# Graph network on one core: the search for slot starts on 125 partitions, with one row tile in its first group and the load of x moved ahead of the weights

## The chip, the core and the metric

The kernel runs on one core of a Trainium2 chip. The core has a matrix engine (PE, with its weight loads listed as PEld), a vector engine (DVE), a scalar engine (ACT), GpSimd (POOL) and a sync engine (SP) that here only issues DMAs. SP and ACT each have a hardware DMA queue; POOL has a software queue, used here for indirect gathers. All of them feed the same 16 DMA engines. Operands lie in an on-chip memory of 128 partitions, and matmul results in PSUM banks.

The metric is the device time of one execution in microseconds (us). The median of three runs before the change is 1657.53 us (1656.67 to 1657.77). The profiled execution took 1656.98 us; its instructions cover a span of 1655.2 us, so 1.8 us lie around the span. A change of less than 0.2% (3.3 us) can't be told from none.

## The reference

There are 6250 nodes with 64 features and 200,000 edges `(src, dst)`, sorted by `dst`, with 16 attributes each.

```
mean = segment_sum(x[src], dst) / max(count, 1)          # two SAGE layers
h    = relu(mean @ W_l1.T + b_l1 + x @ W_r1.T)
out  = mean(h) @ W_l2.T + b_l2 + h @ W_r2.T
x    = layernorm(x + out)
...                                                      # then three message layers
m    = concat([x[dst], x[src], edge_attr]) @ W.T + b
h    = relu(segment_sum(m, dst))                         # a batchnorm and a relu between layers
x    = layernorm(x + h)
```

Every layer sums over the neighbours of a node, with the same edges.

## The kernel before

**The plan.** The kernel turns the edges once into a dense matrix of counts (fp8, in 13 column tiles of 512 destinations; `adj8` in HBM), and each layer is then a matrix product with it (`aggregate`, L650). To build a tile (`build`, L920), the sorted edges are cut into windows of a few destinations. A window owns some *slots* of 128 edges. For a slot, DVE makes two one-hot matrices (L620: `lo` from the source, `rhs` from source and destination), PE multiplies them into a PSUM bank (L958), and ACT writes the counts out as fp8 (L965, L970). 128 slots share one *row tile* `t`: one indirect gather fetches 128 edges for each of the 128 slots (`rows`, L886), and DVE, ACT and PE make keys of it (L893 to L905). There are 21 row tiles (`R = 21`).

**The search.** For the gather, each slot needs the position of its first edge. Source and destination are packed into one integer per edge (`combine`, L791 and L792) and stored to HBM as one list, `cmb_d` (L797). The edges lie as 128 partitions of 1562, and the 64 left over form a rest `tl`, loaded, packed and stored by itself (L778, L779, L798). Four samples per partition (`smp`) are compared with every slot's threshold (`thr`, L815), PE counts the samples below (L820), and DVE turns the count into the position of the nearest sample by six small operations (L822 to L827). That is `near_samples`. An indirect gather then fetches the block of 456 edges behind the sample (L829), DVE counts in it (L838) and adds up the start (L840 to L842): `first_edges`. Row tiles are searched in five groups, `SEARCH`, of 3, 5, 5, 5 and 4 (the last of the 22 columns holds the starts for the edge attributes). An entry `(a, b, t0, t1)` says: group `a..b` takes its samples when row tile `t0` is reached, and finishes when `t1` is reached.

**The rest of the front.** `load_weights` (L585) issues 25 DMAs on SP, transposes the weights on PE (L589) and copies them out on ACT (L590). Behind it, x is loaded into `res` on SP: L872 for the 48 whole blocks of 128 nodes (1536 KB in rows of 256 bytes), L873 for the last 106 nodes. `split` (L626) divides x into three bf16 parts, in 13 pieces of four blocks (the last has one): two ACT casts and three DVE operations each (L629 to L633). The first `first_layer` product needs all 13.

**Order.** A planner places each engine's instructions, mostly as soon as it takes their inputs to be ready; `pin` keeps an instruction behind everything written before it for its engine. Pinned before the change are the comparisons L815, the gathers L829 and L886 and the counts L838. Each engine then runs its queue strictly in order.

**The bias.** `first_layer` adds `b_l2` to `res` (L729), once per tile. The loop over tiles of the second SAGE layer (L1064) reads `res` at L1073.

```
SEARCH = ((0, 3, 0, 0), (3, 8, 1, 2), (8, 13, 3, 4), (13, 18, 4, 5), (18, 99, 5, 6))
            search(0)
            load_weights()
```

Of the kernel before, what the change touches and what calls it, by code (L numbers as in the profile page):

```python
# [22 lines left out]
P = 128  # L23
# [393 lines left out]
SEARCH = ((0, 3, 0, 0), (3, 8, 1, 2), (8, 13, 3, 4), (13, 18, 4, 5), (18, 99, 5, 6))  # L417
NEAR = 456
# [58 lines left out]
def gnn_kernel(ctx: ExitStack, tc: tile.TileContext, x, src, dst, ea, W_l1, b_l1, W_r1, W_l2, b_l2, W_r2,  # L477
# [19 lines left out]
    EC1 = E // P  # L497
    TAIL = E - EC1 * P

# [21 lines left out]
    assert PADE >= P * EAG * 0 and EC1 * P + TAIL == E  # L521
# [30 lines left out]
    with ExitStack() as fast:  # L552
# [153 lines left out]
        def first_layer(psa1, a, j):  # L706
# [17 lines left out]
            for i in range(nb):  # L724
# [4 lines left out]
            nc.vector.tensor_tensor(res[:, bs: bs + nb, :], res[:, bs: bs + nb, :],  # L729
                                    bl2.unsqueeze(1).to_broadcast([P, nb, D]), ALU.add)  # L730
# [3 lines left out]
        with ExitStack() as bld:  # L734
# [19 lines left out]
            cmb = scratch[:, : 4 * EC1].bitcast(I32)  # L754
            sr = scratch[:, 4 * EC1: 8 * EC1].bitcast(I32)
            thr = scratch[:, 8 * EC1: 8 * EC1 + 4 * P * (R + 1)].bitcast(F32)
            most = max(min(b, R + 1) - a for a, b, *_ in SEARCH)
            size = 2 * NSMP * P * most
            less = [room[:, i * size: (i + 1) * size].bitcast(BF16).rearrange("p (q s) -> p q s", q=NSMP) for i in range(2)]
# [11 lines left out]
            tl = pp.tile([TAIL, 2], I32, name="tl")  # L771
            nc.sync.dma_start(cmb, dst[0: EC1 * P].rearrange("(p c) -> p c", p=P))
            nc.scalar.dma_start(sr, src[0: EC1 * P].rearrange("(p c) -> p c", p=P))
            t_ap = t_dram.ap() if hasattr(t_dram, "ap") else t_dram
            early = SEARCH[0][1] * P
            nc.scalar.dma_start(thr[:, :early], t_ap[:, :early].to_broadcast([P, early]))
            nc.scalar.dma_start(thr[:, early:], t_ap[:, early:].to_broadcast([P, P * (R + 1) - early]))
            nc.scalar.dma_start(tl[:, 0:1], dst[EC1 * P:].rearrange("(p c) -> p c", c=1))  # L778
            nc.scalar.dma_start(tl[:, 1:2], src[EC1 * P:].rearrange("(p c) -> p c", c=1))  # L779
            nc.scalar.dma_start(tab, c_dram.ap() if hasattr(c_dram, "ap") else c_dram)  # L780
            nc.scalar.dma_start(etab, e_dram.ap() if hasattr(e_dram, "ap") else e_dram)
            nc.gpsimd.memset(pad, 8191 << SBITS | TAG)
            one = pp.tile([P, 1], BF16, name="one")
            nc.gpsimd.memset(one, 1.0)

            gap = -(-EC1 // NSMP)
            smp = pp.tile([P, NSMP], I32, name="smp")
            every = slice(0, (NSMP - 1) * gap + 1, gap)

            def combine(to, d_, s_):  # L790
                nc.vector.tensor_scalar(to, d_, TAG >> SBITS, SBITS, ALU.bitwise_or, ALU.logical_shift_left)  # L791
                nc.vector.tensor_tensor(to, to, s_, ALU.bitwise_or)  # L792
# [3 lines left out]
            combine(tl[:, 0:1], tl[:, 0:1], tl[:, 1:2])  # L796
            nc.sync.dma_start(cmb_d[0: EC1 * P, :].rearrange("(p c) o -> p (c o)", p=P), cmb)  # L797
            nc.scalar.dma_start(cmb_d[EC1 * P: E, :], tl[:, 0:1])  # L798
            nc.scalar.dma_start(cmb_d[E: NCMB, :].rearrange("(p c) o -> p (c o)", p=64), pad[:64, :])

            blks = [spare(NEAR).bitcast(I32) for _ in range(most)]
            junk = spare(NEAR // 2).bitcast(BF16)
            ci = pp.tile([P, R + 1], I32, name="ci")
            cp = pp.tile([P, R + 1], I32, name="cp")
# [4 lines left out]
            def near_samples(g):  # L809


                t0, t1 = SEARCH[g][0], min(SEARCH[g][1], R + 1)
                s, n = slice(t0, t1), (t1 - t0) * P
                for q in range(NSMP):
                    pin(nc.vector.tensor_scalar(less[g % 2][:, q, :n], thr[:, t0 * P: t1 * P],  # L815
                                                smp[:, q: q + 1].bitcast(F32), None, ALU.is_gt))
                c1 = psm.tile([P, R + 1], F32, name="lin")
                for t in range(t0, t1):
                    for q in range(NSMP):
                        nc.tensor.matmul(c1[:, t: t + 1], less[g % 2][:, q, (t - t0) * P: (t - t0 + 1) * P], one,  # L820
                                         start=(q == 0), stop=(q == NSMP - 1))
                nc.vector.tensor_scalar(ci[:, s], c1[:, s], -1.0, 0.0, ALU.add, ALU.max)  # L822
                nc.vector.tensor_single_scalar(cp[:, s], ci[:, s], 2, ALU.logical_shift_right)
                nc.vector.tensor_single_scalar(ci[:, s], ci[:, s], NSMP - 1, ALU.bitwise_and)
                nc.vector.tensor_single_scalar(near[:, s], cp[:, s], float(EC1), ALU.mult)
                nc.vector.scalar_tensor_tensor(near[:, s], ci[:, s], float(gap), near[:, s], ALU.mult, ALU.add)
                nc.vector.tensor_copy(pos[:, s], near[:, s])  # L827
                for t in range(t0, t1):
                    pin(nc.gpsimd.indirect_dma_start(  # L829
                        out=blks[t - t0], out_offset=None, in_=cmb_d[:, :],  # L830
                        in_offset=bass.IndirectOffsetOnAxis(ap=pos[:, t: t + 1], axis=0)))

            def first_edges(g):

                t0, t1 = SEARCH[g][0], min(SEARCH[g][1], R + 1)
                s = slice(t0, t1)
                for t in range(t0, t1):
                    pin(nc.vector.tensor_scalar(junk, blks[t - t0].bitcast(F32), tab[:, 0, t: t + 1], None,  # L838
                                                ALU.is_lt, ALU.add, accum_out=c2[:, t: t + 1]))
                nc.vector.tensor_add(near[:, s], near[:, s], c2[:, s])  # L840
                nc.vector.tensor_add(near[:, s], near[:, s], tab[:, 1, s])
                nc.vector.tensor_copy(start_i[:, s], near[:, s])  # L842
# [12 lines left out]
            def search(t):  # L855
                for g, (_, _, t0, t1) in enumerate(SEARCH):
                    if t == t1:
                        if t0 == t1:
                            near_samples(g)
# [3 lines left out]
                for g, (_, _, t0, t1) in enumerate(SEARCH):  # L863
                    if t == t0 < t1:
                        near_samples(g)

            search(0)
            load_weights()


            nc.vector.memset(res[:, NB - 1, :], 0.0)
            nc.sync.dma_start(res[:, : NB - 1, :], x[0: (NB - 1) * P, :].rearrange("(b p) d -> p b d", p=P))  # L872
            nc.sync.dma_start(res[:LASTB, NB - 1, :], x[(NB - 1) * P:, :])  # L873
            nc.gpsimd.memset(parts[0][:, :, 3 * D: 3 * D + 1], 1.0)
            for b in range(0, NB, 4):
                nb = min(4, NB - b)
                split(parts[0][:, b: b + nb, :], res[:, b: b + nb, :], nb)
# [3 lines left out]
            def columns(t):  # L881
# [7 lines left out]
                if t:  # L889
                    search(t)  # L890
# [173 lines left out]
            for j in range(NT):  # L1064
# [8 lines left out]
                nc.vector.tensor_add(v[:, :nb, :], v[:, :nb, :], res[:, bs: bs + nb, :])  # L1073
                layer_norm(res[:, bs: bs + nb, :], v[:, :nb, :], nb)
# [155 lines left out]
```

## Time and profile before

| View | Value |
|---|---|
| Median of 3 runs | 1657.53 us |
| Profiled execution | 1656.98 us |
| Its span | 1655.2 us, mean granted PE clock 0.964 |
| Busy in the span | PE 1496.9, PEld 1379.9, DVE 920.0, ACT 578.4, POOL 117.0 us |
| Chain that ended last | PE 62%, DVE 21%, ACT 7%, issue 5%, DMA 3% |
| `dst` issued on SP, first DVE operation on it | 0.74 us, 6.95 us |
| Packed edges stored (L797 issued) | 12.93 us |
| First block gather (L829), first row gather (L886) | 23.29 us, 31.17 us |
| First key operation (L893), first one-hot (L620) | 38.09 us, 40.78 us |
| First slot product (L958) | 42.18 us |
| DVE operations of the splits of x | 46.42 to 70.5 us |
| Additions of `b_l2` (L729) | 13, of 0.42 us, from 145.1 to 622.3 us |

The page divides the span into 40 slices of 41.4 us; the front with which the change deals is the first of them, and the building of the matrix ends near 600 us. Busy times of single instructions overlap a little on DVE. A transfer's time from issue to landing includes its place in the queue.

### The profile page before, as it was taken

How to read it: one execution, taken by the hardware profiler on the slowest of the kernel's cores; microseconds unless marked ns; L12 is line 12 of the kernel's file. 1: busy time of each engine (PE TensorE's matmuls, PEld its weight loads, DVE VectorE, ACT ScalarE, POOL GpSimd, SP SyncE). 2: the span in 40 equal slices, each digit the busy share in tenths (PEclk: the TensorE clock that was granted, in tenths of full speed). 3: DMA queues.
4: the chain of work that ended last, by engine and by line, in shares of the span. 5: the costliest groups of instructions: out<-in, count | busy, mean ns of one | idle time of the engine just before them, and what ended most of it. 6: DMA issues, size and time to landing. Idle time of an engine off the chain costs nothing.

```text
span 1655.2 us, 38577 instructions
## 1 busy us (share of the span) xinstructions
PE 1496.9 (90%) x17135; PEld 1379.9 (83%) x17135; DVE 920.0 (56%) x1581; ACT 578.4 (35%) x1088; POOL 117.0 (7%) x72
## 2 busy tenths in 40 slices
PE   1586789899998989999999999999999999999997
PEld 0475668788887779889999888888899999899997
DVE  2999999998898733897888610001340100442122
ACT  1625466776885721454455300000220000310000
POOL 2024200360001010000000000000000000000000
PEclk9697899999999999999999999999899999899999
DMA  5021332032130373344534444442324542345450
GB/s 163 11 107 55 110 96 85 12 154 83 80 157 2 150 287 159 137 150 183 200 133 142 172 165 179 187 173 99 156 117 197 197 194 99 157 178 227 164 186 10
DMA packets 43811, 228.10 MB, mean 138 GB/s; under 512 B 22978, under 2 KB 30210, under 8 KB 35826
## 3 DMA queue, kind: packets, MB, share of 16 engines
q1 hardware_dynamic: 37058, 139.54, 22.4%
q10 hardware_dynamic: 4496, 79.48, 12.2%
q0 software_dynamic: 2080, 6.52, 1.3%
q8 instruction: 136, 2.23, 0.5%
q14 instruction: 41, 0.34, 0.1%
HBM read 183.76 MB, written 41.75 MB: 136 GB/s over the span
## 4 chain that ended last, share of the span: by engine, by line
PE 62%; DVE 21%; ACT 7%; issue 5%; DMA 3%; ACTq 0%; POOL 0%; DVEq 0%; POOLq 0%
PE agg L650 47%; DVE lo L620 7%; PE pair L958 6%; DVE rhs L620 4%; ACT a L965 4%; PE u L1110 2%; PE bank L1025 2%; DVE e L1016 1%; PE agg L657 1%; DVE e L1018 1%; DMA e<-in_edge_attr_dram 1%; DVE nd L675 1%; PE tr L700 1%; PE lin L1131 1%; DMA a<-adj 1%
## 5 line engine op out<-in xcount | busy, mean ns | idle before, releaser
L650 PE MATMUL agg<-parts,a 128*128 128x192 bf16 (+1 forms) x12005 | 1089.8, 246 | 5.6 <-DVE nd L675 1.8
L650 PEld LDWEIGHTS <-a 128*128 128x128 fp8e3 x12005 | 1008.3, 98 | 23.6 <-issue 12.1
L965 ACT ACTIVATE a<-pair 128x784 fp8e3<-128x784 f32 (+3 forms) x355 | 292.3, 890 | 122.8 <-PE pair L958 121.2
L958 PE MATMUL pair<-rhs,lo 128*128 128x147 bf16 (+5 forms) x2569 | 266.2, 244 | 64.0 <-DVE lo L620 30.3
L958 PEld LDWEIGHTS <-lo 128*128 128x128 bf16 x2569 | 196.2, 104 | 119.4 <-issue 52.1
L620 DVE TENSOR_TENSOR rhs<-iota,k 128x1960 bf16<-128x1960 f16 (+15 forms) x240 | 238.9, 1015 | 13.6 <-ACT k L905 11.3
L620 DVE TENSOR_TENSOR lo<-iota,k 128x2048 bf16<-128x2048 f16 x161 | 194.5, 1215 | 0.0
L675 DVE TENSOR_REDUCE z<-agg 128x256 f32<-128x768 f32 (+1 forms) x39 | 35.3, 910 | 282.7 <-PE agg L650 282.4
L620 DVE TENSOR_TENSOR lo<-iota,e_d 128x2048 bf16<-128x2048 f16 (+11 forms) x132 | 130.7, 1010 | 20.6 <-PE bank L1025 19.8
L1025 PE MATMUL bank<-lo,lhs 128*128 128x128 bf16 x1701 | 107.5, 219 | 17.4 <-ACT lhs L1019 12.1
L1025 PEld LDWEIGHTS <-lhs 128*128 128x128 bf16 x1701 | 98.4, 98 | 28.6 <-ACT lhs L1019 19.4
L675 DVE TENSOR_REDUCE nd<-agg 128x256 f32<-128x768 f32 (+1 forms) x26 | 23.4, 904 | 116.0 <-PE agg L650 116.0
L886 POOL DMA_INDIRECT rows<-cmb_d,start_i x21 | 64.8, 3084 | 207.4 <-ACT key L897 167.0
L1118 DVE BATCH_NORM_STATS2 stats<-hr 64x6 f32<-64x512 f32 (+1 forms) x26 | 17.0, 653 | 101.7 <-ACT hr L1133 80.4
L702 ACT COPY mx<-tr 128x512 f32<-128x512 f32 (+1 forms) x26 | 14.6, 562 | 166.9 <-PE tr L700 166.8
L691 ACT ACTIVATE sp_r<-z 128x256 f32<-128x256 f32 (+1 forms) x26 | 10.5, 403 | 171.4 <-DVE z L690 171.4
L1147 ACT ACTIVATE hr<-tr 64x512 f32<-64x512 f32 (+1 forms) x13 | 7.4, 566 | 179.9 <-PE tr L1146 179.9
L1015 ACT CAST lhs<-e 128x512 bf16<-128x512 f32 (+21 forms) x72 | 36.1, 502 | 59.6 <-PE bank L1025 44.6
L1126 POOL TENSOR_TENSOR nd<-res,inv 128x256 f32<-128x256 f32 (+1 forms) x13 | 7.6, 589 | 550.5 <-DVE ln_s L688 339.2
L1019 ACT CAST lhs<-e 128x512 bf16<-128x512 f32 (+21 forms) x72 | 36.4, 505 | 23.1 <-DVE e L1018 22.6
L1016 DVE TENSOR_TENSOR e<-e,lhs 128x512 f32<-128x512 f32 (+21 forms) x72 | 39.4, 550 | 8.9 <-ACT lhs L1015 8.8
L1017 ACT CAST lhs<-e 128x512 bf16<-128x512 f32 (+21 forms) x72 | 36.3, 504 | 22.2 <-DVE e L1016 21.0
(140 smaller groups left out, 819.6 us busy)
## 6 DMA issues: line engine op xcount, KB each, us to landing
a<-adj SPq DMA_DIRECT2D x24, 3136.0 KB, 12.4
a<-adj ACTq DMA_DIRECT2D x24, 3136.0 KB, 11.5
adj<-a SPq DMA_DIRECT2D x12, 3136.0 KB, 9.6
e<-in_edge_attr_dram SPq DMA_DIRECT2D x25, 256.0 KB, 2.7
a<-adj SPq DMA_DIRECT2D x4, 784.0 KB, 4.2
out_dram<-z SPq DMA_DIRECT2D x12, 128.0 KB, 6.5
a<-first_edges ACTq DMA_DIRECT2D x1, 1216.0 KB
e<-in_edge_attr_dram SPq DMA_DIRECT2D x7, 152.0 KB, 3.3
```

What stands on the lines that cost most here:

```text
L620: nc.vector.tensor_tensor(to.rearrange("p g (h two) -> p g h two", two=2), iota[:, :n].rearrange("p (h two) -> p h two", two=2).unsqueeze( ...
L650: nc.tensor.matmul(sums[k][:, i, :n], views[k][:, b, i * P: (i + 1) * P], pt[:, b, :n], start=(b == sources[0] and terms is None and not ( ...
L675: nc.vector.tensor_reduce(to, ps[:, :nb, : 3 * D].rearrange("p b (r d) -> p b d r", r=3), AX.X, ALU.add)
L886: pin(nc.gpsimd.indirect_dma_start(out=rows, out_offset=None, in_=cmb_d[:, :], in_offset=bass.IndirectOffsetOnAxis(ap=start_i[:, t: t + 1] ...
L958: nc.tensor.matmul(pair[:, bank % 2, col: col + wc], lo_hot(t, c), rhs[:, i, :wc], start=first, stop=last)
L965: nc.scalar.activation(av[:, :, o: o + 2 * nd].rearrange("p h (two d) -> p h two d", two=2), pair[:, :, : nd * NB].rearrange("p two (d h) ...
L1015: nc.scalar.copy(lhs[:, :g, 0:EC], r)
L1016: nc.vector.tensor_sub(r, r, lhs[:, :g, 0:EC])
L1017: nc.scalar.copy(lhs[:, :g, EC:2 * EC], r)
L1019: nc.scalar.copy(lhs[:, :g, 2 * EC:3 * EC], r)
L1025: nc.tensor.matmul(ps[:, :P], lhs[:, q, :], oh[:, q % HOT, :], start=(c == 0 and q == 0), stop=(i == last_b[b] and q == g - 1))
L1110: nc.tensor.matmul(u[:, i, :], y[:, i * P: (i + 1) * P], maps[n - 1], start=True, stop=True)
```

## The change

The edges are laid out as `EP = 125` partitions of 1600, the largest number of partitions up to 128 that leaves nothing over and has four samples a whole number of edges apart (`GAP = 400`). The rest `tl` with its loads, its packing and its store goes. Because the samples are now evenly spaced, the position is the count times 400: two DVE operations, both pinned, in place of six. The blocks are 400 edges wide in place of 456.

The groups become 1, 4, 6, 5 and 6 row tiles. The first two both take their samples in `search(-1)`, ahead of everything else, and group 0 is finished there; group 1 is finished at row tile 0, behind the first row gather. The loads of `src`, of the thresholds of the first two groups (`early`, now 640 columns), of `tab` and the store of the padding go on ACT; x goes on SP directly behind `dst`. The store of the packed edges goes on ACT. The weights follow on SP behind x, and behind them the thresholds of the other groups. The splits of x stand in the program around the first two groups: pieces 0 and 1 before `first_edges(0)`, pieces 2 to 4 behind it, pieces 5 to 12 behind the first row gather and `first_edges(1)`.

Last, the addition of `b_l2` moves from `first_layer` to the loop of the second SAGE layer, onto `v`.

```diff
-SEARCH = ((0, 3, 0, 0), (3, 8, 1, 2), (8, 13, 3, 4), (13, 18, 4, 5), (18, 99, 5, 6))
-NEAR = 456
+SEARCH = ((0, 1, -1, -1), (1, 5, -1, 0), (5, 11, 1, 2), (11, 16, 3, 4), (16, 99, 5, 6))
...
-    EC1 = E // P
-    TAIL = E - EC1 * P
+    EP = max(p for p in range(1, P + 1) if E % (p * NSMP) == 0)
+    EC1 = E // EP
+    GAP = EC1 // NSMP
...
-            nc.vector.tensor_tensor(res[:, bs: bs + nb, :], res[:, bs: bs + nb, :],
-                                    bl2.unsqueeze(1).to_broadcast([P, nb, D]), ALU.add)
...
-            nc.sync.dma_start(cmb, dst[0: EC1 * P].rearrange("(p c) -> p c", p=P))
-            nc.scalar.dma_start(sr, src[0: EC1 * P].rearrange("(p c) -> p c", p=P))
...
-            nc.scalar.dma_start(thr[:, early:], t_ap[:, early:].to_broadcast([P, P * (R + 1) - early]))
-            nc.scalar.dma_start(tl[:, 0:1], dst[EC1 * P:].rearrange("(p c) -> p c", c=1))
-            nc.scalar.dma_start(tl[:, 1:2], src[EC1 * P:].rearrange("(p c) -> p c", c=1))
...
+            nc.sync.dma_start(cmb, dst.rearrange("(p c) -> p c", p=EP))
+            nc.scalar.dma_start(sr, src.rearrange("(p c) -> p c", p=EP))
...
+            early = SEARCH[1][1] * P
+            nc.scalar.dma_start(thr[:, :early], t_ap[:, :early].to_broadcast([EP, early]))
+            nc.scalar.dma_start(tab, c_dram.ap() if hasattr(c_dram, "ap") else c_dram)
+            nc.scalar.dma_start(cmb_d[E: NCMB, :].rearrange("(p c) o -> p (c o)", p=64), pad[:64, :])
+
+            nc.vector.memset(res[:, NB - 1, :], 0.0)
+            nc.sync.dma_start(res[:, : NB - 1, :], x[0: (NB - 1) * P, :].rearrange("(b p) d -> p b d", p=P))
+            nc.sync.dma_start(res[:LASTB, NB - 1, :], x[(NB - 1) * P:, :])
...
-            combine(tl[:, 0:1], tl[:, 0:1], tl[:, 1:2])
-            nc.sync.dma_start(cmb_d[0: EC1 * P, :].rearrange("(p c) o -> p (c o)", p=P), cmb)
-            nc.scalar.dma_start(cmb_d[EC1 * P: E, :], tl[:, 0:1])
...
+            nc.scalar.dma_start(cmb_d[0: E, :].rearrange("(p c) o -> p (c o)", p=EP), cmb)
...
-                nc.vector.tensor_scalar(ci[:, s], c1[:, s], -1.0, 0.0, ALU.add, ALU.max)
-                nc.vector.tensor_single_scalar(cp[:, s], ci[:, s], 2, ALU.logical_shift_right)
-                nc.vector.tensor_single_scalar(ci[:, s], ci[:, s], NSMP - 1, ALU.bitwise_and)
-                nc.vector.tensor_single_scalar(near[:, s], cp[:, s], float(EC1), ALU.mult)
-                nc.vector.scalar_tensor_tensor(near[:, s], ci[:, s], float(gap), near[:, s], ALU.mult, ALU.add)
-                nc.vector.tensor_copy(pos[:, s], near[:, s])
+                pin(nc.vector.tensor_scalar(near[:, s], c1[:, s], -1.0, 0.0, ALU.add, ALU.max))
+                pin(nc.vector.tensor_single_scalar(pos[:, s], near[:, s], float(GAP), ALU.mult))
...
             def search(t):
+                if t < 0:
+                    near_samples(0)
+                    near_samples(1)
+                    split_x(0, 2)
+                    first_edges(0)
+                    split_x(2, 5)
+                    return
...
-            search(0)
+            def split_x(c0, c1):
+                for b in range(c0 * 4, min(c1 * 4, NB), 4):
+                    nb = min(4, NB - b)
+                    split(parts[0][:, b: b + nb, :], res[:, b: b + nb, :], nb)
+
+            search(-1)
             load_weights()
...
+            nc.scalar.dma_start(etab, e_dram.ap() if hasattr(e_dram, "ap") else e_dram)
+            nc.sync.dma_start(thr[:, early:], t_ap[:, early:].to_broadcast([EP, P * (R + 1) - early]))
...
-                if t:
-                    search(t)
+                search(t)
+                if t == 0:
+                    split_x(5, NB)
...
+                nc.vector.tensor_tensor(v[:, :nb, :], v[:, :nb, :], bl2.unsqueeze(1).to_broadcast([P, nb, D]), ALU.add)
                 layer_norm(res[:, bs: bs + nb, :], v[:, :nb, :], nb)
```

## The prediction

> **What bounds it now.** I read the slices of the span first, then busy time by stretch, then the chain of waits and the order of time in the first 45 us. DVE carries the building of the matrix, PE the rest:
>
> ```profile
> PE   1586789899998989999999999999999999999997
> DVE  2999999998898733897888610001340100442122
> ```
>
> The sums by stretch (columns: stretch, length, busy PE, PEld, DVE, ACT, POOL with counts, clock, DMA share, GB/s):
>
> ```profile
> 0.00:38.09 38.09, 4.76 (x24) 2.30 (x24) 8.49 (x32) 3.88 (x13) 8.41 (x16) 1.00 0.62 177
> 38.09:230.00 191.91, 134.24 (x1493) 108.87 (x1494) 185.37 (x326) 94.36 (x142) 41.60 (x27) 0.80 0.19 63
> 230.00:300.00 70.00, 67.96 (x753) 59.50 (x753) 67.28 (x98) 45.80 (x69) 7.51 (x4) 1.00 0.30 104
> ```
>
> From the first keys (38.09) to 230 DVE is busy 97% and PE 70%: this stage ends when DVE is through its work. From 230 to 400 both are near full, later PE alone. PE has no slack of its own to give there, so a shift of the first stage passes on to the end. Hence one account decides: **how much later or earlier DVE starts its one-hots, less the DVE work taken from behind that point.** In the front DVE works 8.49 of 38.09 us. Three waits of the chain fill it:
>
> ```profile
> 1.68 10.21 DMA a<-first_edges
> 14.38 7.31 DMA cmb_d<-parts
> 31.17 6.89 DMA rows<-cmb_d,start_i
> ```
>
> The first is the thresholds (1,408 KB on ACT), which hold up the rest's load behind them, and DVE's comparisons behind the rest's packing. The second are the small stores: SP's queue waits for the large store (issued 12.93) until before 17.3, for the padding's until 21.7; the rest's lands at 22.4 (15.57 + 6.8). The third is the first row gather, which runs into the load of x.
>
> **What the change removes behind the first one-hot.** Splits: 12 pieces of 0.415 + 0.417 + 0.284 us and one of 0.62 are 14.0 us of DVE (L630, L632, L633), all behind 46 us. Groups 1 to 4 of the search: comparisons 3 x 1.93 + 1.66 = 7.4; small operations 24 x 0.165 = 4.0; counts 19 x (0.68 + 0.08) = 14.4; tails 12 x 0.165 = 2.0. With the splits 41.9 us. After the change groups 2 to 4 are left (17 tiles): comparisons 2.2 + 1.9 + 2.2 = 6.3 (the slope from 384 to 640 columns, 0.404 to 0.543 us each, carried to 768); small ones 6 x 0.165 = 1.0; counts 17 x 0.70 (400 of 456 columns: between 0.60 and 0.68, I take 0.62, plus 0.08) = 11.9; tails 9 x 0.165 = 1.5: 20.7 us. Add the splits that don't find room in front: none to 13; I take the eight written behind the first row gather, 7 x 1.12 + 0.6 = 8.4. Left 29.1: **12.8 us less** (21.2 if all splits fit, 7.1 if none does).
>
> **When the first one-hot comes.** It was 40.78. Here row and rule part. Bulk loads ran on all 16 engines:
>
> ```profile
> 4.00:5.00 1.00, 0.00 (x0) 0.00 (x0) 0.00 (x0) 0.00 (x0) 0.08 (x1) 1.00 1.00 419
> 1650.00:1651.00 1.00, 0.00 (x0) 0.00 (x0) 0.00 (x0) 0.00 (x0) 0.00 (x0) 0.50 0.12 33
> ```
>
> The first is 26 GB/s for each of 16. By that row 125 partitions cost what 128 do. The rule against it is in the Trainium skill, "DMA: Bandwidth & Descriptors", section "Why a DMA increments its semaphore by 16 and not by 1": a hardware-queue DMA uses the largest number of engines up to 16 that divides the slowest dimension. 125 gives 5, the lowest-numbered ones. The second row bears it out on another odd shape: the last store, of 106 rows (largest divisor 2), runs at a share of 0.12, two sixteenths. Its packets say it too, in the DMA view from 1648 us on:
>
> ```profile
> q1 hardware_dynamic: 108, 0.03, 1.5%
> ```
>
> 106 rows and 2 closing packets; with the store of 512 rows before it the count is 636, so that one took 528 = 512 + 16. No transfer of 125 rows is in this trace, but I go by the rule. The sum by each:
>
> - *All 16 engines.* Inputs at 7.0, packing 3.1 us (6.95 to 10.06), store landed near 15 (before: 4 us), five block gathers at 1.25 us each to 21.5, row gather landed near 25.5, keys and casts 2.7 more (38.09 to 40.78): 28 to 30, **11 us earlier**.
> - *Five engines.* Engines 0 to 4 must carry, at 26 KB/us each: `dst` and `src`, 320 KB per engine, 12.2 us from about 2.9: landed at **15.1**, not 6.95. Early thresholds, 64 KB, 2.5 us. Packing ends at 18.3. Then the store, 160 KB, 6.1 us, beside x, 96 KB per engine at the 13.3 GB/s of its 256-byte rows (219 GB/s of 16 engines from 33 to 37 us): 7.3 us. x queues on these engines behind `dst`. All is through at 15.1 + 2.5 + 7.3 + 6.1 = **31**; the store, in larger packets, near 27[...]. Without the rest's and padding's late stores nothing else is waited for.
>
> On five engines the first block gather starts at 27.5 (before 23.29), the fifth is issued by 33.8. `first_edges(0)` is pinned behind split pieces 0 and 1, so behind x: 31 + 3.2 (1.9 for the first piece's ACT-DVE ping-pong, 1.2 for the second) + 1.3 (one count, tail) = 35.5. Row gather at 36, landed 4 later (3.5 to 4 where nothing crossed it; 6.9 before): keys at 40, first one-hot at 43.
>
> **Queues passed.** x now stands ahead of the 25 weight DMAs on SP. The issue of L873 stood 5.3 us, until 33.6, while x drained to 37.1; so SP comes free about 3.5 us before x ends, at 27.5. 21 weight DMAs at 0.62 us (start to start at 24.6 to 27.1 us), 2.2 to land, 1.3 for the last transposes and copies: 44. These stand on PE and ACT ahead of the first key transposes and casts, as before (there done at 27.4, hidden under the wait for x). Cover gone, they set the first one-hot: **45**, 4.2 later. ACT's splits may stand behind the copies too, hence eight pieces behind. The late thresholds (1,344 KB, on five engines 10.3 us) land by 58; before, the second comparisons ran at 75.07, behind the first row tile's one-hots. POOL's row gather stands behind five block gathers in place of three: 2.5 us, under the wait for x.
>
> **Bias.** Removed additions in the DVE-bound part: three by 300 us, 1.3 us gained; the ten later ones lie under PE, 0 to 1. Added: 13 x 0.42 less a short one = 5.2 us of DVE from 660 to 950, where DVE is 82% busy and PE 94%, and DVE on the chain nearly half of the time: between 0 and 5.2, I take half, 2.5. Net +1.2. The packing on 1600 columns costs 0.1, in the account above.
>
> **Sum.** +4.2 (later start) - 12.8 (work gone or done in the wait) + 1.2 = -7.4 us. Against the profiled execution's own 1656.98 that is 1649.6; the median is 0.55 above that execution. Forecast **1650 us**. Its own range: first one-hot 42 to 50 and splits left between none and all: 1640 to 1656.
>
> **Rivals.**
>
> *Sixteen engines after all.* For: every large transfer in the trace has 128 rows and full share. Against: 106 rows took two. -11.3 - 12.8 + 1.2 = -22.9: 1634.
>
> *Weights in front of the keys.* If SP, or one of its first weight DMAs, is held until x has fully landed, all the rest follows: in this trace SP's DMAs do wait for landings of earlier ones (for `src` 3.8 us at the sixth, for the padding's store 3.3):
>
> ```profile
> SPq L596 <- DMA a<-in_src_dram: 3.8, 1, 3.8
> SPq L601 <- DMA cmb_d<-parts: 3.3, 1, 3.3
> ```
>
> From x at 31 the weights took 19.3 us before (7.10 to 26.4): 50.3, copies and key 2.5: one-hot at 53, +12.2 - 12.8 + 1.2 = +0.6. From 53 on the change loses, one for one. x landed at 36 instead, because its short rows go slower beside the store or the block gathers, makes it 58: +5.6, 1662 to 1663. Against: some weight DMAs can go before the block, and the two late small stores, which cost SP 3.3 us, are gone.
>
> *The gain stays inside.* If PE, not DVE, sets the end of the building (97% from 230), DVE time saved behind the first one-hot only lowers its share: +4.2 - 8 + 1.2 to 0: about 1655, within 0.2%.
>
> **Chances.** Five engines and a gain near the forecast 0.42; sixteen engines 0.14; weights ahead, slower 0.32; gain inside 0.12. For faster by over 0.2% (under 1654.2; 3.3 us is what can be told from no change): most of the first and the second, 0.52. Within: 0.16. Slower: 0.32. Since both signs carry weight, the range for 8 in 10 spans the cases: 1633 to 1664.
>
> **What will show it.** Five engines: DVE's first packing near 15 us, DMA share near 0.3 while `dst` and `src` load, some 130 GB/s beside x; 125 rows with 16 closings would be 141 packets, with 5 they are 130. x landing near 31: the first split then. Weights: the last copy L590 ahead of the first L905, near 44; above 51 it's the slower rival. Passing on: DVE near 97% from the first one-hot to about 222 us, and the end of the building as much earlier as the account says. Bias: the stretch from 660 to 950 up to 5 us longer. Wrong would be: packing at 7 us (sixteen engines); the first one-hot in place and the end not moved (PE sets it); comparisons of group 2 waiting for thresholds.

## The result, and the profile after

The changed kernel takes **1670.53 us** (median of 6 runs, 1668.96 to 1671.77) against 1657.51 for the kernel before beside it: ratio 1.0077, 95% interval 1.0064 to 1.0089. It is 13.0 us slower; the forecast was 1650, the range 1633 to 1664. The profiled spans differ by 12.0 us (1667.2 to 1655.2). The mean granted PE clock was 0.967 in the slower kernel and 0.964 in the faster one, so the clock isn't the cause.

Below, line numbers are the changed kernel's: row gather L878, its first key operation `hi` L886, block gather L818, one-hots L619, reciprocal L712 (one per column tile, when its counts are complete). The same two rows of slices as before the change:

```profile
PE   1476779899998989999999999999999999999997
DVE  2889989998897832897788721101241110342122
```

DVE falls short in the slices just behind the front, and PE with it. The same three stretches by busy time (stretch, length, PE, PEld, DVE, ACT, POOL with counts, clock, DMA share, GB/s):

```profile
0.00:38.09 38.09, 3.02 (x23) 1.60 (x23) 9.60 (x33) 5.17 (x14) 6.84 (x15) 1.00 0.54 134
38.09:230.00 191.91, 126.58 (x1461) 102.97 (x1462) 174.90 (x298) 90.52 (x139) 47.11 (x29) 0.86 0.21 67
230.00:300.00 70.00, 63.41 (x683) 55.72 (x683) 61.62 (x86) 44.70 (x65) 5.71 (x4) 0.95 0.31 104
```

In the last one no loss was expected at all, yet DVE worked 5.7 us less there (67.28 before) and PE 4.6. Now the front, in the chain of waits (start, us, what):

```profile
0.74 18.21 DMA a<-in_dst_dram
...
20.28 1.84 DVE a L788
...
22.14 0.28 ACTq L792
...
22.46 10.48 DMA cmb_d<-parts
```

The inputs land at 18.95 (before 6.95), packing ends at 22.1, and the first block gather starts at 33.84 (before 23.29). The first row gather starts at 40.41 (31.17), its `hi` at 47.10 (38.09), the first one-hot at 58.26 (40.78). So 9 us of delay became 17.5 between keys and one-hot. What DVE waited for at `hi` is told by that line's view, first of the kernel before (L893), then of the changed one (columns: what ended the idle time, us, times):

```profile
engine op xcount: duration ns min/median/max, first and last start us, forms
L893 DVE TENSOR_SCALAR hi<-rows x21: 211/218/227, 38.1 to 529.8; 128x128 int32<-128x128 int32 x21
its engine sat idle before it (us, times) until:
  DMA rows<-cmb_d,start_i: 7.2, 1
```

```profile
L886 DVE TENSOR_SCALAR hi<-rows x21: 214/221/228, 47.1 to 540.9; 128x128 int32<-128x128 int32 x21
its engine sat idle before it (us, times) until:
  DMA rows<-cmb_d,start_i: 16.2, 4
```

Before, DVE waited once, for the first row tile, when there was nothing else to do. Now the first tile's wait is gone (splits fill it), and there are others. DVE in order of time (start, us, instruction, idle time before it and what ended it):

```profile
56.71 0.23 DVE L886 TENSOR_SCALAR hi<-rows 128x128 int32<-128x128 int32 x1 [5.77 <-DMA rows<-cmb_d,start_i]
...
104.95 0.23 DVE L886 TENSOR_SCALAR hi<-rows 128x128 int32<-128x128 int32 x1 [3.42 <-DMA rows<-cmb_d,start_i]
...
246.94 0.23 DVE L886 TENSOR_SCALAR hi<-rows 128x128 int32<-128x128 int32 x1 [6.04 <-DMA rows<-cmb_d,start_i]
```

At 57 and at 247 us the planner has put the keys of a *later* row tile in DVE's queue ahead of one-hots of an earlier one: tile 1's ahead of tile 0's, and tile 10's ahead of tile 8's (eight `lo` operations make a tile; 64 stand before 246.94). The later tile's gather has not landed, and DVE stops. At 57 us ACT's queue is in the same order: tile 0's last cast, L898, stands behind tile 1's first, L890, which needs DVE's work on tile 1:

```profile
57.38 0.30 ACT L890 CAST key<-rows 128x128 f32<-128x128 int32 x1 [6.35 <-DVE rows L889]
57.58 0.58 ACT L898 CAST k<-lin 128x512 f16<-128x512 f32 x1
```

The wait at 105 us is another: there the one-hots of tiles 0 and 1 are all done, tile 2's keys are the next thing needed, and their gather went late (95.82); only five counts of the search, 0.63 us each, stand behind it. In all 5.77 + 3.42 + 6.04 = **15.2 us** of a DVE that the stage can't spare. The reciprocals, before and after:

```profile
L713 DVE RECIPROCAL inv<-inv x13: 162/169/178, 118.5 to 610.4; 128x4 f32<-128x4 f32 x12, 128x1 f32<-128x1 f32 x1
```

```profile
L712 DVE RECIPROCAL inv<-inv x13: 164/171/178, 128.7 to 621.8; 128x4 f32<-128x4 f32 x12, 128x1 f32<-128x1 f32 x1
```

The last one of the building comes at 621.78 in place of 610.36, 11.4 later: all but 0.6 us of the difference between the spans arises before that.

### The profile page after: what moved, and what is told of

It reads as the page before. It is cut to its first block, busy times and chain, and to the rows that moved or that the text cites. A ratio compares the mean times of both kernels' runs of the same rounds, so it can differ in the third digit from the quotient of the medians.

```text
span 1667.2 us, 38564 instructions
## 1 busy us (share of the span) xinstructions
PE 1494.8 (90%) x17135; PEld 1379.2 (83%) x17135; DVE 916.7 (55%) x1559; ACT 579.1 (35%) x1088; POOL 88.1 (5%) x72
## 4 chain that ended last, share of the span: by engine, by line
PE 59%; DVE 16%; issue 11%; ACT 7%; DMA 5%; POOL 2%; ACTq 0%; DVEq 0%; POOLq 0%
PE agg L649 46%; DVE lo L619 6%; PE pair L951 4%; ACT a L958 4%; DVE rhs L619 2%; PE u L1104 2%; PE bank L1018 2%; DMA a<-adj 1%; DVE e L1009 1%; POOL parts L818 1%; PE agg L656 1%; DVE e L1011 1%; DMA a<-in_dst_dram 1%; DVE nd L674 1%; DMA rows<-cmb_d,start_i 1%
## 5 line engine op out<-in xcount | busy, mean ns | idle before, releaser
L951 PE MATMUL pair<-rhs,lo 128*128 128x147 bf16 (+5 forms) x2569 | 259.5, 240 | 64.8 <-DVE lo L619 35.2
L951 PEld LDWEIGHTS <-lo 128*128 128x128 bf16 x2569 | 192.3, 102 | 116.4 <-DVE lo L619 47.9
L619 DVE TENSOR_TENSOR rhs<-iota,k 128x1960 bf16<-128x1960 f16 (+15 forms) x240 | 239.1, 1017 | 19.5 <-ACT k L898 15.1
L619 DVE TENSOR_TENSOR lo<-iota,k 128x2048 bf16<-128x2048 f16 x161 | 194.8, 1217 | 0.0
L619 DVE TENSOR_TENSOR lo<-iota,e_d 128x2048 bf16<-128x2048 f16 (+11 forms) x132 | 130.8, 1011 | 19.2 <-PE bank L1018 18.4
L1018 PE MATMUL bank<-lo,lhs 128*128 128x128 bf16 x1701 | 107.5, 219 | 16.7 <-ACT lhs L1012 11.4
L878 POOL DMA_INDIRECT rows<-cmb_d,start_i x21 | 35.3, 1683 | 235.1 <-ACT key L890 227.0
L1009 DVE TENSOR_TENSOR e<-e,lhs 128x512 f32<-128x512 f32 (+21 forms) x72 | 39.4, 551 | 8.6 <-ACT lhs L1008 8.3
L1011 DVE TENSOR_TENSOR e<-e,lhs 128x512 f32<-128x512 f32 (+21 forms) x72 | 39.3, 547 | 6.7 <-ACT lhs L1010 6.0
```

Source lines behind the costliest of these rows:

```text
L619: nc.vector.tensor_tensor(to.rearrange("p g (h two) -> p g h two", two=2), iota[:, :n].rearrange("p (h two) -> p h two", two=2).unsqueeze( ...
L878: pin(nc.gpsimd.indirect_dma_start(out=rows, out_offset=None, in_=cmb_d[:, :], in_offset=bass.IndirectOffsetOnAxis(ap=start_i[:, t: t + 1] ...
L951: nc.tensor.matmul(pair[:, bank % 2, col: col + wc], lo_hot(t, c), rhs[:, i, :wc], start=first, stop=last)
L1009: nc.vector.tensor_sub(r, r, lhs[:, :g, 0:EC])
L1011: nc.vector.tensor_sub(r, r, lhs[:, :g, EC:2 * EC])
L1018: nc.tensor.matmul(ps[:, :P], lhs[:, q, :], oh[:, q % HOT, :], start=(c == 0 and q == 0), stop=(i == last_b[b] and q == g - 1))
```

## The experiments

"One-hot" is the start of the first one, "built" that of the last reciprocal of the building, from each profile. The experiments follow in the order of the table; a name with `a_` starts from the changed kernel, one with `b_` from the kernel before. The kernel before ran beside each group of runs, at medians of 1657.5 to 1660.1 us, so times of different groups are compared by the ratio. Before: one-hot 40.8, built 610.4; after: 58.3 and 621.8.

| Kernel | Median us (ratio to before, 95%) | One-hot | Built |
|---|---|---|---|
| `a_112_13` | 1656.42 (0.9983, 0.9973 to 0.9994) | 42.1 | 608.8 |
| `b_125_3` | 1674.35 (1.0094, 1.0077 to 1.0111) | 56.0 | 624.6 |
| `a_pad_first` | 1670.3 (1.0066, 1.0049 to 1.0082) | 57.7 | 622.8 |
| `a_group3` | 1656.44 (0.9987, 0.9979 to 0.9994) | 49.9 | 608.7 |
| `a_pin_hi` | 1655.67 (0.9982, 0.9975 to 0.9990) | 52.5 | 607.1 |
| `a_112_13_pin_hi` | 1642.77 (0.9900, 0.9884 to 0.9917) | 39.9 | 596.1 |
| `a_112_13_group3` | 1642.79 (0.9901, 0.9883 to 0.9919) | 37.6 | 594.5 |
| `a_bias` | 1671.02 (1.0074, 1.0058 to 1.0090) | 58.2 | 623.3 |
| `b_x_early` | 1652.77 (0.9962, 0.9948 to 0.9975) | 44.2 | 605.2 |
| `a_x_late` | 1674.17 (1.0092, 1.0077 to 1.0108) | 61.8 | 627.5 |
| `a_112_13_group3_x_late` | 1655.32 (0.9972, 0.9964 to 0.9980) | 50.0 | 606.9 |
| `b_x_early_act` | 1651.49 (0.9952, 0.9939 to 0.9966) | 44.7 | 603.9 |

**125 rows cut into 112 and 13.** In the changed kernel, each transfer of 125 rows (`dst`, `src`, both parts of the thresholds, the store) is made of two:

```diff
-            nc.sync.dma_start(cmb, dst.rearrange("(p c) -> p c", p=EP))
...
+            CUT = ((0, 112), (112, EP))
+            for a, b in CUT:
+                nc.sync.dma_start(cmb[a:b], dst[a * EC1: b * EC1].rearrange("(p c) -> p c", p=b - a))
```

> The changed kernel, with each transfer of 125 rows cut into one of 112 (divisible by 16) and one of 13. Theory 'five engines': a transfer of 125 rows runs on 5 of 16 DMA engines, and that delays the front. Then the first packing comes near 8 to 9 us (18.97 in the changed kernel), the first block gather near 20 (33.84), the first one-hot at 42 to 46 (58.26), and the time is 12 to 15 us shorter than the changed kernel's: 1656 to 1659. Rival 'order later on': the front is absorbed by DVE's saved work and the loss lies in a wait near 241 us; then the packing may come earlier, but the time stays within 3 us of 1670.

The stretch from 16 to 19 us, busy times as above, the changed kernel first, then the one with the cut:

```profile
16.00:19.00 3.00, 0.00 (x0) 0.00 (x0) 0.03 (x1) 0.00 (x0) 0.00 (x0) 1.00 0.31 123
```

```profile
16.00:19.00 3.00, 0.51 (x13) 0.43 (x13) 0.86 (x5) 0.81 (x3) 0.00 (x0) 1.00 1.08 330
```

0.31 is five sixteenths, at 123 GB/s, for what is left of the inputs. With the cut these are long in (first packing at 9.99 in place of 18.97), and what runs from 16 to 19 us is mostly the store with x, on all engines at 330. Packing ends at 13.15 in place of 22.11, and the first block gather starts at 21.02, the first one-hot at 42.1. The time falls by 14 us. (The planner also put the padding's store ahead of the large one here; the next experiment but one shows that this is worth nothing.) But of 16.2 us earlier at the one-hot only 13.0 are left when the matrix is built, and this kernel still waits at `hi`, 14.0 us in all. The longest wait:

```profile
231.95 0.23 DVE L891 TENSOR_SCALAR hi<-rows 128x128 int32<-128x128 int32 x1 [7.67 <-DMA rows<-cmb_d,start_i]
```

**The same put upon the kernel before.** Its loads of `dst` and `src` and the store of the edges are cut into 125 and 3 rows in place of one transfer of 128.

```diff
-            nc.sync.dma_start(cmb, dst[0: EC1 * P].rearrange("(p c) -> p c", p=P))
...
+            CUT = ((0, 125), (125, P))
+            for a, b in CUT:
+                nc.sync.dma_start(cmb[a:b], dst[a * EC1: b * EC1].rearrange("(p c) -> p c", p=b - a))
```

> The kernel before, with only the loads of dst and src and the store of the packed edges cut into 125 and 3 rows (128 partitions of 1562 as before). Theory 'five engines': dst and src land near 15 instead of 6.95 us, the first block gather starts at 30 to 33 (23.29), the first one-hot at 48 to 51 (40.78), and as no DVE work is saved the whole delay passes on: 1665 to 1668. Rival 'sixteen engines': first packing at 7 to 8 us and 1657 to 1659.

The same stretch of 3 us here:

```profile
16.00:19.00 3.00, 0.00 (x0) 0.00 (x0) 0.00 (x0) 0.00 (x0) 0.00 (x0) 1.00 0.33 119
```

The one-hot comes 15.2 us later, the building ends 14.2 later and the time is 16 longer. So the number of rows alone does it (each transfer was cut in two in the run above as well, and that one gained), and in this stage a later start is passed on almost whole. The size was underrated by 8 us: the rest's load and packing wait in ACT's queue behind the slow ones (until 25.99), and its store behind them (first block gather 36.70).

**The padding's store first.** The chain names the small store of the padding as the last before the gathers. It was pinned ahead of the large one.

```diff
-            nc.scalar.dma_start(cmb_d[0: E, :].rearrange("(p c) o -> p (c o)", p=EP), cmb)
+            pin(nc.scalar.dma_start(cmb_d[0: E, :].rearrange("(p c) o -> p (c o)", p=EP), cmb))
```

> The changed kernel, with the store of the packed edges pinned behind the small store of the padding, which was issued behind it at 22.46 us and seemed to hold the first block gather until 33.84. Theory 'the small store holds the gather': the gather starts at 29 to 31, the first one-hot 3 to 4 us earlier, 1666 to 1668. Rival 'the large store itself lands at 33': gather at 33 to 34 as before, no change, 1670.

It now goes at 2.56 us, and the first block gather still starts at 33.61 (33.84). So the small store is not what holds them. The large one, issued at 22.14 (here 22.30) on five engines beside x, is what is left for the gathers to wait for; the name in the chain was that of the release seen last.

**The groups of before.** 125 rows on five engines stay; only the groups and what follows from them change.

```diff
-SEARCH = ((0, 1, -1, -1), (1, 5, -1, 0), (5, 11, 1, 2), (11, 16, 3, 4), (16, 99, 5, 6))
+SEARCH = ((0, 3, -1, -1), (3, 8, 1, 2), (8, 13, 3, 4), (13, 18, 4, 5), (18, 99, 5, 6))
...
-            early = SEARCH[1][1] * P
+            early = 5 * P
...
-                    near_samples(1)
```

> The changed kernel with the groups of the kernel before (3, 5, 5, 5, 4; the first sampled and finished in front, the second at row tiles 1 and 2). Theory 'the first keys wait for the second row tile': in the changed kernel the cast L898 of row tile 0 stands on ACT behind the cast L890 of row tile 1, whose start is found only in group 1 and whose gather lands at 56.71. With three row tiles in the first group both row gathers go at once: first one-hot at 46 to 50 (58.26), some 3 to 7 us of DVE work comes back behind it, 1664 to 1668. Rival 'weights hold the first keys': first one-hot above 55, time 1670 or more.

14 us less, though the edges land no sooner (first block gather 33.95), and some 8 us below the theory's range, which counted only the wait at 57 us. POOL in order of time, the changed kernel first, then this one:

```profile
40.41 0.94 POOL L878 DMA_INDIRECT rows<-cmb_d,start_i  x1 [0.30 <-issue]
46.59 4.98 POOL L878 DMA_INDIRECT rows<-cmb_d,start_i  x1 [5.24 <-DVE parts L632]
```

```profile
41.92 1.41 POOL L877 DMA_INDIRECT rows<-cmb_d,start_i  x1 [4.34 <-DVE parts L632]
43.64 1.00 POOL L877 DMA_INDIRECT rows<-cmb_d,start_i  x1 [0.30 <-issue]
```

With one row tile in front its gather goes 1.5 us sooner, but that of the second, whose start belongs to the next group, goes 3 us later, takes POOL 4.98 us and lands at 56.7. With three in front both are there by the time DVE has the keys to make; DVE's waits at `hi` are 0.9 us in all.

**Only the place of the keys.** In the changed kernel, groups and five engines untouched, `hi` and `dl` of row tiles 1 and 10 are pinned behind the one-hots that stand before them in the program (`id` leaves an operation where the planner puts it).

```diff
-                nc.vector.tensor_scalar(hi, rows, 7, 63, ALU.logical_shift_right, ALU.bitwise_and)
+                late = pin if t in (1, 10) else id; late(nc.vector.tensor_scalar(hi, rows, 7, 63, ALU.logical_shift_right, ALU.bitwise_and))
...
-                nc.vector.tensor_scalar(dl, rows, SBITS, (1 << SBITS) - 1, ALU.logical_shift_right, ALU.bitwise_and)
+                late(nc.vector.tensor_scalar(dl, rows, SBITS, (1 << SBITS) - 1, ALU.logical_shift_right, ALU.bitwise_and))
```

> The changed kernel, but the first key operations of row tiles 1 and 10 (hi and dl) are pinned, so that they stand in DVE's queue behind the one-hots of the row tile before, no longer ahead of them. Five engines stay. Theory A (half of the loss is DVE's queue: twice it stands 6 us at hi for a row gather that is only needed 128 slots later): the first one-hot at about 52.5 us in place of 58.26, the wait of 6.04 us at 247 gone, the time 1659 to 1663, about 10 less than the 1670.5 of the change; a late key chain may give 2 or 3 of it back. Theory B (only the late landing of the edges counts, and the waits are filled again or hidden under PE): 1668 to 1671.

DVE in order of time:

```profile
50.65 0.28 DVE L892 TENSOR_SCALAR key<-key,tab 128x128 f32<-128x128 f32 x1
51.04 0.23 DVE L631 TENSOR_TENSOR sp_r<-sp_r,parts 128x64 f32<-128x64 f32 x1
51.30 0.27 DVE L632 CAST parts<-sp_r 128x64 bf16<-128x64 f32 x1
52.46 0.21 DVE L619 TENSOR_TENSOR rhs<-iota,k 128x98 bf16<-128x98 f16 x1 [0.89 <-ACT k L898]
```

DVE's part of tile 0's keys is done at 50.9 in both kernels; here the cast L898 follows on ACT at 51.77 and then the one-hots, where the changed kernel stood until 56.71. And the view of `hi`:

```profile
its engine sat idle before it (us, times) until:
  DMA rows<-cmb_d,start_i: 1.1, 1
```

All three waits are gone, that at 105 us too, whose instruction is not pinned: DVE now comes to it 8.3 us behind the start of its gather (88.97 to 97.23), where in the changed kernel it came after 5.7 (95.82 to 101.5). By the ratios (0.9982 to 1.0077) this is 15.7 us less: as much as the waits, more than theory A allowed, which counted two of them and something given back. Moving the keys of two row tiles back in the queues turns a kernel that is 13 us slower than before into one that is 3 us faster (0.18%, just under the 0.2% that counts as a difference here).

**Both.** The cut with the pins, and the cut with the groups of before (both diffs as above).

> The same pins, with every transfer of 125 rows cut into 112 and 13 (all 16 engines). Its group of one row tile in front stays. Theory A: the first one-hot near 36.5 us (it was 42.06 with the cut alone) and no wait near 232: 1645 to 1650. Theory B (from 230 us on PE sets the end of the building, so a start earlier than about 42 is not passed on): 1654 to 1657, as with the cut alone (1656.4).

> The changed kernel with both edits that gained 14 us each: transfers cut into 112 and 13 rows, and the groups of before (3, 5, 5, 5, 4). Theory A (the two are separate: the edges land 13 us earlier, and the keys no longer stand in front of the one-hots): first one-hot near 37 us, no wait of over 2 us of DVE between 200 and 260, 1642 to 1648. Theory B (PE's limit, or both edits cure the same 14 us): 1653 to 1657.

Both take 1642.8 us, **15.7 us less than the kernel before**, the best versions found. From 1670.5, the cut gave 14 and the waits 14 to 15; together they give 27.7, so they are separate. Two readings fell, and the pinned one came out under the 1645 to 1650 of its theory A. Theory B of both, that PE's limit keeps an earlier start inside, would have left 1654 to 1657. And for the pinned one the one-hot was to come near 36.5; it came at 39.9, since the last splits stand between the keys in DVE's queue (`hi` at 34.6, the last key operation at 38.1). A group of one row tile in front, then, buys nothing over three even without its waits: its one-hot is 2.3 us later.

**The bias back.** The addition of `b_l2` is put back in `first_layer`, in the changed kernel.

```diff
+            nc.vector.tensor_tensor(res[:, bs: bs + nb, :], res[:, bs: bs + nb, :],
+                                    bl2.unsqueeze(1).to_broadcast([P, nb, D]), ALU.add)
...
-                nc.vector.tensor_tensor(v[:, :nb, :], v[:, :nb, :], bl2.unsqueeze(1).to_broadcast([P, nb, D]), ALU.add)
```

> The changed kernel with the addition of b_l2 back in first_layer. If the bias cost what the prediction says (1.3 us gained while DVE builds, 2.5 lost from 660 to 950), the time is 1 to 1.5 us under the 1670.5 of the change, and the stretch from the end of the building to the end of the second SAGE layer 2 to 3 us shorter. If it costs nothing there, as the two traces suggest (+0.3 us), the time is 1670 to 1672.

No difference. Busy times from 660 to 950 us, the changed kernel, then this one:

```profile
660.00:950.00 290.00, 273.38 (x3722) 262.07 (x3720) 242.23 (x426) 141.95 (x371) 1.19 (x2) 1.00 0.49 178
```

```profile
660.00:950.00 290.00, 273.29 (x3727) 262.39 (x3725) 237.71 (x410) 140.81 (x367) 1.19 (x2) 1.00 0.49 177
```

DVE has 4.5 us more to do with the addition there, PE none, and from the last reciprocal of the building to the cast of `ok_i`, just behind the second SAGE layer, the three kernels take 343.2 (before), 342.9 (after) and 343.1 us (this one).

**x early, alone.** In the kernel before, the load of x goes directly behind `dst` on SP; its lines behind the weights go.

```diff
             nc.sync.dma_start(cmb, dst[0: EC1 * P].rearrange("(p c) -> p c", p=P))
             nc.scalar.dma_start(sr, src[0: EC1 * P].rearrange("(p c) -> p c", p=P))
+            nc.vector.memset(res[:, NB - 1, :], 0.0)
+            nc.sync.dma_start(res[:, : NB - 1, :], x[0: (NB - 1) * P, :].rearrange("(b p) d -> p b d", p=P))
+            nc.sync.dma_start(res[:LASTB, NB - 1, :], x[(NB - 1) * P:, :])
```

> The kernel before with nothing changed but the load of x, issued on SP directly behind dst (in front of the store of the edges and of the weights); 128 partitions, the rest, the groups and the bias stay. Theory (the useful part of the change is the splits of x, 14 us of DVE, done in waits of the front): the first one-hot 2 to 4 us later than 40.78, since x shares the DMA engines with dst and src, all splits ahead of it, the end 9 to 12 us earlier: 1646 to 1650. Rival (x in front pushes the weights and with them the keys back as far as it wins): first one-hot near 50, 1655 to 1659.

0.38%, or 6.3 us: the direction of the theory, less than its size. The one-hot comes 3.4 later as expected, with all splits ahead of it, but from there to the second reciprocal only 9.5 us are saved (it comes 6.1 earlier, 231.0 to 224.9, and the start is 3.4 later), not 14. DVE's busy time in this stretch falls by 11.1 us (from 185.3 to 174.2, idle times taken off), and it idles 1.6 us longer, 1.38 of them at an `hi` at 89 us. So the splits were worth 11 us; the last experiment, without such waits, saves 11.8 in the same stretch. The edges are stored late here, as SP's queue shows (start, us, instruction):

```profile
22.04 0.32 SPq L776 DMA_DIRECT2D res<-in_x_dram  x1
22.46 0.36 SPq L800 DMA_DIRECT2D cmb_d<-a  x1
```

SP holds the second load of x back until the first has landed (ACT's first cast of it starts at 21.99), and the store, whose data is packed near 10.2, behind it.

**x late.** x behind the store of the edges, on ACT, first in the changed kernel and then in the best version.

```diff
-            nc.sync.dma_start(res[:, : NB - 1, :], x[0: (NB - 1) * P, :].rearrange("(b p) d -> p b d", p=P))
-            nc.sync.dma_start(res[:LASTB, NB - 1, :], x[(NB - 1) * P:, :])
...
             nc.scalar.dma_start(cmb_d[0: E, :].rearrange("(p c) o -> p (c o)", p=EP), cmb)
+            pin(nc.scalar.dma_start(res[:, : NB - 1, :], x[0: (NB - 1) * P, :].rearrange("(b p) d -> p b d", p=P)))
+            pin(nc.scalar.dma_start(res[:LASTB, NB - 1, :], x[(NB - 1) * P:, :]))
```

> The changed kernel, but x is issued on ACT behind the store of the packed edges, so that nothing of 16 engines runs beside dst and src. Theory (x took bandwidth of the five engines while they loaded dst and src; this is the 3.8 us by which packing was later than predicted): first packing near 15 us in place of 18.97, first block gather 3 to 4 us earlier, first one-hot 54 to 56, 1665 to 1668. Rival (five engines are bound by their own rate, x or not): packing at 18 to 19 and, with x now beside the store, 1670 to 1674.

> The best version (cut transfers, groups of before) with x behind the store of the edges, on ACT. If the path to the first row gather sets the first one-hot (packing 3 us earlier, near 10): first one-hot near 35 us, 1639 to 1642. If the splits, which stand in DVE's queue ahead of the counts, then wait for x: first one-hot 38 to 40, 1643 to 1646 (1642.8 without this edit).

Neither gains. The first takes the rival's time and can't be told from the changed kernel (1.0092 to 1.0077, intervals overlap); the second loses. In the first the packing does start 2.1 us sooner (16.87), so x had cost that much while it ran beside the five engines; then x is late. DVE in order of time:

```profile
16.87 0.17 DVE L785 TENSOR_SCALAR smp<-a 125x4 int32<-125x4 int32 x1 [15.66 <-DMA a<-in_dst_dram]
...
41.96 0.43 DVE L629 TENSOR_TENSOR sp_r<-res,parts 128x256 f32<-128x256 f32 x1 [17.93 <-ACT parts L628]
```

The splits, which stand ahead of the counts, wait 17.9 us for it. In the best version x costs about 12 us in this place (0.9972 to 0.9901), one-hot 12.4 later. Neither theory had the size: there x, on ACT behind the store, is issued at 20.09, and its first cast starts at 34.8.

**x early and the store on ACT.** As the kernel with x early, and the large store moved off SP:

```diff
-            nc.sync.dma_start(cmb_d[0: EC1 * P, :].rearrange("(p c) o -> p (c o)", p=P), cmb)
+            nc.scalar.dma_start(cmb_d[0: EC1 * P, :].rearrange("(p c) o -> p (c o)", p=P), cmb)
```

> The kernel before with x directly behind dst and, in addition, the store of the packed edges on ACT in place of SP, where it stood behind x's second load until 22.46 us. 128 partitions, the rest, the groups and the bias of before. Theory (these two moves are all that is useful in the change; the 125 partitions bring nothing once they are cut for 16 engines): first block gather at 20 to 23 us (28.43 without the move of the store), first one-hot 37 to 40, 1643 to 1647, like the best version (1642.8). Rival (the rest's own load, packing and store still hold the first gather, so 125 partitions without it are worth something): first block gather 25 to 28, 1649 to 1652.

1651.5 us, by the rival. The store goes at 10.32, but the block gathers start at 27.94, since the small stores now stand last (ACT in order of time):

```profile
10.32 0.33 ACTq L800 DMA_DIRECT2D cmb_d<-a  x1
14.63 0.48 ACTq L801 DMA_DIRECT2D cmb_d<-tl  x1
24.45 0.47 ACTq L802 DMA_DIRECT2D cmb_d<-parts  x1
```

Against x early alone the gathers start 0.5 us sooner, and no gain is clear of noise (0.9952 to 0.9962). So this run doesn't tell the rest's own price from that of the padding's store, which could have gone early. Whether 128 partitions with a rest could equal the best version is open.

## Why the prediction was wrong, point by point

**Right: five engines.** The share of 0.31 for 125 rows is five sixteenths, as forecast, and the cuts into 112 and 13 and into 125 and 3 rows show from both sides what it costs.

**Right: what sets the stage.** A shift at the first one-hot is passed on (14.2 of 15.2 us in the kernel with 125 and 3), and work taken from DVE counts. The rival in which the gain stays inside fell with the two versions at 1642.8.

**The step that failed** is "Hence one account decides: how much later or earlier DVE starts its one-hots, less the DVE work taken from behind that point." The account followed the first row tile only. It took DVE as filled from its first one-hot on, because the kernel before was busy 97% there, and had no term for the second tile: whose start now belongs to another group, whose gather is issued 6 us behind the first, and whose keys the planner may place ahead of the first tile's one-hots. The changed kernel needs a third term, of waits in DVE's own queue, which the prediction put at nothing. The pinned kernel gives the account without it. The second reciprocal, before and pinned:

```profile
L713 DVE RECIPROCAL inv<-inv x1: 177/177/177, 231.0 to 231.0; 128x4 f32<-128x4 f32 x1
```

```profile
L712 DVE RECIPROCAL inv<-inv x1: 176/176/176, 227.0 to 227.0; 128x4 f32<-128x4 f32 x1
```

The start is 52.5 in place of 40.8, **+11.7**; the reciprocal is 4.0 earlier, so work behind the start is **-15.7**; sum -4.0, and the time is 0.9982 of before, -2.9. With the waits, **+15.2**, the sum is +11.2 against +11.4 at the end of the building.

**Mis-sized: the later start**, +4.2 predicted, +11.7 without the wait. Packing ended at 22.1, not 18.3. With x away it still ended at 20.1, so x took 2 of these 3.8 us; the rest is probably that the thresholds share the five engines with `dst` and `src` and don't run behind them, which no run tested apart. The store took 10.8 us to the release of the gathers, so these started at 33.8, not 27.5. Waiting for x before the counts was overrated: the first cast of x starts at 26.35, not 31, and the row gather at 40.4 where 33.8 + 8.5 was the working. (The rate of x had been read a little high: 219 GB/s holds from 33 to 36 us; to 37 it is 205.) But DVE came to the first `hi` 6.7 us behind that gather, not 4. It didn't wait for the landing there; splits and the counts of the second group stood in front. The keys took another 5.4 to the one-hot, since splits stand between them on DVE and ACT.

**Mis-sized: the work behind the start**, -12.8 predicted for eight pieces left. All 13 were done in front, for which the working had -21.2; it came to -15.7. Part of the difference is the splits, put at 14.0 us: with x early alone they were worth 11. In the trace splits of 0.42 us follow each other at 0.34; 39 operations that overlap by 0.08 make 3 us (an estimate), which the sum of durations counted twice. The other 2 to 3 us were not traced. Against the forecast this term is -2.9 off and the start +7.5; that they cancel in part is luck.

**Weights in front of the keys** had the chance for slower, and its time, 1662, was on the right side for a wrong cause. The last copy of the weights was done at 46.4, ahead of the first `hi` at 47.1 and of the first key cast on ACT at 49.5, so no key waited for them.

**The bias** was given +1.2; no cost could be measured.

## What to carry to other kernels

When a first group is made smaller so that its result comes sooner, follow the *second* item too: if its gather comes late and its consumer stands in an in-order queue ahead of the first item's work, the engine stops there. Look for waits on the engine that bounds the stage, far from the edit as well (here at 247 us, for an edit near 20), and try moving the waiting instruction first. The planner's order at 247 us had changed with the groups, not with the transfers: the kernels with the cut alone (7.67 us) and without it (6.04) both have the wait. Choose the rows of a large transfer with an eye to how many engines share it, and cut off a remainder as here: 125 rows into 112, a multiple of 16, and 13.

## What the runs showed of the hardware

- 125 rows ran at a share of 0.31 to 0.33 and about 120 GB/s (16 to 19 us). As long as x ran beside them the other engines were busy too: from 4 to 12 us the share was 1.09 at 208 GB/s with 125 rows, and 1.04 at 232 with 112 and 13. But the inputs were in at 18.97 with 125 rows and at 9.99 with the cut.
- With x early alone SP issued the second load of x only at 22.04, when the first had landed (21.99), and a store behind it that was ready at 10.2 waited too.
- DVE operations recorded at 0.42 us each followed each other at 0.34, so summed durations overrate what an edit saves: 14.0 us of splits by the sum, 11 by DVE's busy time.
- The second row gather took POOL 4.97 to 4.98 us in all seven kernels with one row tile in front, five engines or sixteen, where the first took 0.94 to 0.96. In those with three in front it took 0.94 to 1.07. The cause is open.
